# A12 B21 of a product of two weight matrices in seven inner products on top of A11 B11, and the products with B0 and G's in another order

## The chip, the cores and the metric

The kernel runs on one core of a Trainium2 chip (trn2). The metric is the device time in microseconds of one execution; a profiled execution gives in addition a trace, whose span runs from the first to the last instruction of the program. Engines are named as in the profile: PE is TensorE, PEld its weight loads, DVE is VectorE, ACT ScalarE, POOL GpSimd, SP the queue that issues most of the loads.

## The reference

`x` is 8 x 256 x 1024 in float32. Two layers follow each other, each adding a linear map and a low-rank one to its input:

```
x = x + x @ W0.T + 0.5 * (x @ A0[i0[b]]) @ B0.T
x = x + x @ W1.T + bias + 2.0 * (x @ A1[i1[b]]) @ B1[i1[b]]
```

W0 and W1 are 1024 x 1024. A0 is 5 x 1024 x 32, B0 1024 x 32, A1 32 x 1024 x 16, B1 32 x 16 x 1024; `i0` and `i1` hold an index for each batch.

## The kernel before

The kernel first builds M = (I + W0.T)(I + W1.T), a 1024 x 1024 product of the weights alone, and then multiplies each x by M. Everything is in float32. Both levels use a scheme with seven instead of eight block products (Strassen's, in Winograd's form). Outside, the weights are cut into blocks A11 to A22 and B11 to B22 of 512 x 512, and M comes out as m11, m12, m21, m22 (tiles of 128 x 4 x 512). The first two of the outer products are P1 = A11 B11 and P2 = A12 B21; m11 is their sum, and P1 is used for all the other blocks. `w_groups` holds one `Blocks` for each of the four row tiles of 128 rows; its methods `product6`, `product7`, `product5`, `product3` and `product4` make the other outer products of a row tile directly, four matmuls of 128 x 512 each. Row tiles 0 and 1 are done so, rows 2 and 3 by `Chain`, which makes its outer products in the inner form, seven products of 256 columns (`product`, `keep`, `form`, L515 to L594).

The inner form: `product` (L509 to L558 and around) takes four quarters of the left operand and sums of them (`z_sums`, four VectorE additions), and quarters of the right operand and sums of them (`Operand.sums`, four more). Each of its seven products is two matmuls of 128 x 256 into half a PSUM bank (`slot`); seven slots fill a set of four banks, `sets[0]` being banks 0 to 3 and `sets[1]` banks 4 to 7. Slots can be loaded beforehand and accumulated upon ("loaded"). `keep` copies a set out with four ACT copies, and `form` makes the four quarters of the result with five VectorE additions.

The work is put in order by hand (`manual_schedule`): each engine runs its instructions in the order of the program text, and waits for what each needs. At the start that order is:

- SP's queue: W1 comes as four blocks `wq[h, i]` of 512 x 512, each in four loads (the first in eight), W0 as eight row blocks in two halves of 512 columns (`load_w0(k, 0)`, then `load_w0(k, 1)`). The order is wq[0,0] with the first four W0 blocks between its halves, wq[0,1], the other four W0 blocks, wq[1,0], wq[1,1], `load_b0`, and the second halves of W0. "Third block" and "fourth block" below are wq[1,0] and wq[1,1].
- VectorE turns each block of W1 into `w1T` with stream transposes (`turn_w1`, L225) and adds the identity to the diagonals (L233; for h = 1 POOL does that).
- TensorE warms up with 15 matmuls (L918), makes P1 in two halves (`first`, L951) into banks 0 to 3, which ACT copies into m22 (`keep_p1`, L300), then P2 directly on top of the same banks (`product2`, 16 matmuls of 128 x 512, L286), which ACT copies into m11 (L310). Between these copies ACT issues the eight loads of A1's rows (`load_a1`, L198), three with each row tile.
- Then TensorE makes G = A1.T W0 in two halves (`prepare_down(h)`, L701), the product of B0 with W1 (`prepare_up`, L676, both halves, then `finish_up`, L690), the product of B0 and A1 (`prepare_cross`, L715), and goes on with `product6` of row tile 0. `finish_down` (L728 to L737) folds the cross product through bank 7, has ACT copy it out (L731), and transposes G in two fours of transposes, the second into bank 7.
- VectorE meanwhile makes the sums of the right operand, `sums_w1_first` (L359, L360), those of the left operand of row tile 0 (`w_groups[0].sums`, L272 to L279), and `sums_w1_last` (L365, L367). ACT then starts the inner sums of two right operands, `w_ops["t2"].sums_dma()` and `w_ops["t1"].sums_dma()`: three multiplications each (L431) into `units`, to which POOL's DMAs add.

Of the kernel before, what the change touches and what calls it, by code (L numbers as in the profile page):

```python
# [10 lines left out]
ALU = mybir.AluOpType  # L11
# [9 lines left out]
P = 128  # L21
NH = 512
# [5 lines left out]
NWARM = 15  # L28
NV7 = 7
# [3 lines left out]
NU = 2  # L33
NLOW = 4
NQ = NH // 2
NB = 4
NX = 2
# [5 lines left out]
def kernel(  # L43
# [179 lines left out]
    def turn_w1(wq, h: int, k: int, lo: int = 0, hi: int = NR):  # L223
        cols = slice(h * NH + lo * SQ, h * NH + hi * SQ)
        nc.vector.transpose(  # L225
            w1T[:, k, cols].rearrange("p (t q) -> p t q", q=SQ),
            wq[:, lo:hi].rearrange("p t (q m) -> p m t q", m=NB)[:, k % NB],
        )
# [18 lines left out]
    def new_bank():  # L247
        ring.append(ring.pop(0))
        return ring[-1]
# [225 lines left out]
    def quarters(x):  # L475
        return x[:, 0:2, 0:P], x[:, 2:4, 0:P], x[:, 0:2, P:T], x[:, 2:4, P:T]

    def z_sums(x, z):
        x11, x12, x21, x22 = x
        nc.vector.tensor_tensor(z[0], x21, x22, ALU.add)  # L480
        nc.vector.tensor_tensor(z[1], z[0], x11, ALU.subtract)
        nc.vector.tensor_tensor(z[2], x11, x21, ALU.subtract)
        nc.vector.tensor_tensor(z[3], x12, z[1], ALU.subtract)


    SLOT = {2: 0, 3: 1, 4: 2, 5: 3, 7: 4, 1: 5, 6: 6}
# [3 lines left out]
    def slot(ps, i: int):  # L490
        n, pos = BANK[i]
        return ps[n][:, pos * NQ : (pos + 1) * NQ]
# [78 lines left out]
    def form(v, ps=None, dst=None):  # L571
# [21 lines left out]
        nc.vector.tensor_tensor(mid, src_two(3, 0), two(1), ALU.add)  # L593
        nc.vector.tensor_tensor(d[:, 3 * NQ : 4 * NQ], src(5), at(6), ALU.add)  # L594

    m12 = {}

    def sums_m(m: int):
# [5 lines left out]
    class Chain:  # L604
# [33 lines left out]
            z_sums(self.q(name), self.z[name])  # L638

        def preload(self):  # L640

            p = m22[:, self.tiles, :].rearrange("p m (h n) -> p (m h) n", h=2)
            for i, part in ((2, 0), (4, 2), (5, 3)):
                nc.scalar.copy(slot(self.X, i), p[:, part])
            nc.vector.tensor_tensor(slot(self.X, 3), p[:, 1], p[:, 3], ALU.subtract)
            for i in (1, 7):
                nc.vector.memset(slot(self.X, i), 0.0)

        def product(self, ps, name, which, first, low=None):
            product(ps, self.q(name), self.z[name], w_ops[which], first, low=low)  # L650
# [14 lines left out]
            nc.vector.tensor_tensor(t[which], a, b, op)  # L665


    def prepare_up():
        tile = work[:, 4 * NH : 6 * NH]
        part = [tile[:, h * NH : (h + 1) * NH] for h in range(NO)]  # L670
        for h in range(NO):
            cols = slice(h * NH, (h + 1) * NH)
            pm = new_bank()
            for k in range(NK):
                g = k % 4
                nc.tensor.matmul(  # L676
                    pm[g * R0 : (g + 1) * R0, :],
                    b0[:, k, :],
                    w1T[:, k, cols],
                    start=(k < 4),  # L680
                    stop=(k >= NK - 4),
                )
            nc.scalar.copy(part[h], pm)
        return part

    def finish_up(part):
        for h in range(NO):
            cols = slice(h * NH, (h + 1) * NH)
            pm = new_bank()
            nc.tensor.matmul(  # L690
                pm, fold.rearrange("p u r -> p (u r)"), part[h], start=True, stop=True
            )
            for i in range(NU):
                nc.scalar.copy(ups[i][:, cols], pm)

    gT = [work[:, (6 + h) * NH : (7 + h) * NH] for h in range(NO)]

    def prepare_down(h: int):
        pm = new_bank()
        for k in range(NK):  # L700
            nc.tensor.matmul(  # L701
                pm,
                a1[:, k].rearrange("p b r -> p (b r)"),
                w0n[:, k, h * NH : (h + 1) * NH],
                start=(k == 0),
                stop=(k == NK - 1),
            )
        nc.scalar.copy(gT[h], pm)

    def prepare_cross():  # L710

        pe = banks[7][:, 0:P]
        for k in range(NK):
            g = k % 4
            nc.tensor.matmul(  # L715
                pe[g * R0 : (g + 1) * R0, :],
                b0[:, k, :],
                a1[:, k].rearrange("p b r -> p (b r)"),
                start=(k < 4),
                stop=(k >= NK - 4),  # L720
            )
        part = work[:, 4 * NH : 4 * NH + P]
        nc.scalar.copy(part, pe)
# [170 lines left out]
    with tc.manual_schedule(engines=ORDERED):  # L894
# [10 lines left out]
        load_w1(wq[0, 1], 0, 1)  # L905
        for k in range(NB, NK):
            load_w0(k, 0)
        for i in range(2):
            wq[1, i] = new_w1(1, i)
            load_w1(wq[1, i], 1, i)  # L910
        load_b0()
        for k in range(NK):
            load_w0(k, 1)
        nc.scalar.copy(s_all[:, 0:R0], ident[:, 0:R0])

        pw = banks[6][:, 0:P]
        for _ in range(NWARM):
            nc.tensor.matmul(pw, ident, ident, start=True, stop=True)  # L918
        raw0, raw1 = load_indices(idx0, 0), load_indices(idx1, 1)
        nc.gpsimd.memset(scale, L1_SCALING)  # L920
        for half in range(2):
# [27 lines left out]
        def first(g, k: int, n: int):  # L949
            cols = slice(n * NH // 2, (n + 1) * NH // 2)  # L950
            nc.tensor.matmul(  # L951
                g.p1[:, cols],
                g.a[0][:, k, :],
                w1T[:, k, cols],
                start=False,
                stop=(k == NB - 1),
                skip_group_check=True,
            )

        for k in range(NB):  # L960
            turn_w1(wq[0, 0], 0, k, 0, mid)
            diag_w0(k)
            for g in w_groups:
                first(g, k, 0)
        for k in range(NB):
            turn_w1(wq[0, 0], 0, k, mid, NR)
        for m, g in enumerate(w_groups):
            for k in range(NB):
                first(g, k, 1)
            g.keep_p1(m22[:, m, :])  # L970
        fixed0, fixed1 = fix_indices(raw0, N0, 0), fix_indices(raw1, N1, 1)
        for k in range(NB, NK):
            turn_w1(wq[0, 1], 0, k)
        for m, g in enumerate(w_groups):
            for b in range(3 * m, min(3 * m + 3, B)):
                load_a1(b)
            g.product2(m11[:, m, :])
        for k in range(NB):
            turn_w1(wq[1, 0], 1, k)
        for k in range(NB):  # L980
            turn_w1(wq[1, 1], 1, NB + k)
        for k in range(NB, NK):
            diag_w0(k)
        for k in range(NB):
            sums_w1_first(k)
        prepare_down(0)
        part = prepare_up()
        w_groups[0].sums()
        sums_w1_last()
        finish_up(part)  # L990
        prepare_down(1)
        prepare_cross()
        for which in ("t2", "t1"):
            w_ops[which].sums_dma()

# [285 lines left out]
```

## Time and profile before

| | us |
|---|---|
| median of 3 runs | 336.21 (335.87 to 336.40) |
| the profiled execution, its own time | 336.54 |
| its span | 334.8 |
| TensorE busy in the span | 329.6 (98%) |
| VectorE busy | 246.2 (74%) |
| ACT busy | 61.3 |
| POOL busy | 67.9 |

The granted TensorE clock was 0.999 of full speed. The stretch that the change touches lies between the start and 61 us. Busy times by engine there, from the view by windows: from 22.4 to 31.8 us TensorE was busy for 9.40, VectorE for 0.03; from 42.8 to 56.8, 14.00 and 13.79 us. A record of a float32 matmul in the trace is half of one matmul of the program, so 16 matmuls show as x32. "Busy" of TensorE includes the modelled end of a pipelined matmul; the time for one is best taken from a row of the chain, as its length over its count.

### The profile page before, as it was taken

To read this page: it belongs to the slowest core of one execution; us is meant where nothing else is said; L and a number is where in the kernel's file an instruction comes from. 1 tells how busy PE (TensorE), PEld (TensorE's weight loads), DVE (VectorE), ACT (ScalarE), POOL (GpSimd) and SP (SyncE) were. 2 spreads that over 40 slices of the span, in tenths; PEclk is the share of its full clock that TensorE was granted. 3 is DMA by queue.
4 is the path that set the end of the run, shared out by engine and by line. 5 is a ranking of instruction groups with operands and counts; after the bars stand their busy time and mean duration, and the time that the engine had idled before them with its cause. 6 is when DMAs were issued, how large, how long until landed. Compare 5 with 4: busy or idle time off the path is not lost.

```text
span 334.8 us, 4443 instructions
## 1 busy us (share of the span) xinstructions
PE 329.6 (98%) x1496; PEld 245.1 (73%) x1496; DVE 246.2 (74%) x466; ACT 61.3 (18%) x128; POOL 67.9 (20%) x125
## 2 busy tenths in 40 slices
PE   8999999999999999999999999999999999999996
PEld 8774434544488877888877887877888777788875
DVE  5752697159899999999997856985675986323964
ACT  1022043300034132440001330001331001322000
POOL 7001261540042232771023100012200010000000
PEclk9999999999999999999999999999999999999999
DMA  7949982990062980786277300275500121100113
GB/s 211 199 133 186 271 191 46 168 173 14 0 95 63 194 137 14 113 133 104 95 191 204 79 2 0 74 222 148 116 10 0 63 96 63 64 2 0 63 65 126
DMA packets 66399, 34.53 MB, mean 103 GB/s; under 512 B 47300, under 2 KB 61124, under 8 KB 66376
## 3 DMA queue, kind: packets, MB, share of 16 engines
q1 hardware_dynamic: 56520, 21.13, 27.9%
q0 software_dynamic: 7680, 12.59, 17.4%
q10 hardware_dynamic: 2176, 0.52, 1.0%
q8 instruction: 12, 0.20, 0.2%
q14 instruction: 11, 0.09, 0.1%
HBM read 19.55 MB, written 8.39 MB: 83 GB/s over the span
## 4 chain that ended last, share of the span: by engine, by line
PE 94%; DMA 2%; SPq 1%; DVE 1%; issue 0%; ACT 0%; DVEq 0%
PE bank L523 66%; PE bank L286 14%; PE bank L747 4%; PE bank L701 4%; DMA units<-in_L_cond_W_dram 2%; PE bank L951 2%; PE bank L676 1%; PE bank L765 1%; SPq L170 1%; DVE w1T L225 1%; PE bank L690 1%; SPq L178 1%; DVE w1T L233 0%; PE bank L736 0%; PE bank L715 0%
## 5 line engine op out<-in xcount | busy, mean ns | idle before, releaser
L509 DVE TENSOR_TENSOR work<-bank,work 128x512 f32<-128x512 f32 (+1 forms) x56 | 32.7, 620 | 19.0 <-PE bank L523 18.8
L505 ACT COPY work<-bank 128x512 f32<-128x512 f32 (+1 forms) x56 | 25.8, 548 | 43.0 <-PE bank L523 42.6
L225 DVE STREAM_TRANSPOSE w1T<-units 128x512 f32<-128x512 f32 (+1 forms) x20 | 17.3, 901 | 18.0 <-DMA units<-in_L_cond_W_dram 17.9
L888 POOL DMA_DIRECT2D out_dram<-work x12 | 9.0, 752 | 100.6 <-DVE work L594 100.6
L523 PE MATMUL bank<-w0n,w1T 128*128 128x256 f32 x104 | 24.6, 384 | 0.0
L755 ACT ACTIVATE a<-bank,shift,scale 128x256 f32<-128x256 f32 x8 | 4.5, 564 | 103.3 <-PE bank L747 103.3
L523 PEld LDWEIGHTS bank<-w0n,w1T 128*128 128x128 f32 x104 | 19.3, 190 | 4.1 <-issue 1.7
L523 PE MATMUL bank<-w0n,m 128*128 128x256 f32 x88 | 21.2, 384 | 0.0
L523 PE MATMUL bank<-w1T,s_all 128*128 128x256 f32 x80 | 20.2, 379 | 0.0
L238 DVE STREAM_TRANSPOSE units<-units 128x512 f32<-128x512 f32 x32 | 19.9, 676 | 0.2
L523 PEld LDWEIGHTS bank<-w0n,m 128*128 128x128 f32 x88 | 16.4, 190 | 3.4 <-issue 1.4
L523 PE MATMUL bank<-tw,m 128*128 128x256 f32 x68 | 17.5, 382 | 0.0
L523 PEld LDWEIGHTS bank<-w1T,s_all 128*128 128x128 f32 x80 | 15.2, 190 | 2.1
L523 PE MATMUL bank<-tw,s_all 128*128 128x256 f32 x64 | 16.1, 379 | 0.0
L747 PE MATMUL bank<-units,down 128*64 128x256 f32 x128 | 15.6, 385 | 0.0
L523 PE MATMUL bank<-m,units 128*128 128x256 f32 x64 | 15.1, 379 | 0.0
L951 PE MATMUL bank<-w1T,w0n 128*128 128x256 f32 x64 | 14.5, 383 | 0.5 <-DVE w1T L233 0.5
L523 PEld LDWEIGHTS bank<-tw,m 128*128 128x128 f32 x68 | 12.8, 190 | 2.4 <-issue 0.7
L523 PE MATMUL bank<-w0n,s_all 128*128 128x256 f32 x56 | 14.4, 379 | 0.0
L286 PE MATMUL bank<-tw,s_all 128*128 128x512 f32 x32 | 14.3, 595 | 0.0
L951 PEld LDWEIGHTS bank<-w1T,w0n 128*128 128x128 f32 x64 | 12.3, 196 | 2.4 <-DVE w1T L233 1.3
L701 PE MATMUL bank<-w0n,a 128*128 128x512 f32 x32 | 14.1, 592 | 0.0
(249 smaller groups left out, 646.8 us busy)
## 6 DMA issues: line engine op xcount, KB each, us to landing
units<-in_x_dram SPq DMA_DIRECT2D x128, 64.0 KB, 2.4
out_dram<-work POOLq DMA_DIRECT2D x12, 512.0 KB, 3.5
w0n<-in_L_cond_W_dram SPq DMA_DIRECT2D x16, 256.0 KB, 6.1
units<-in_L_cond_W_dram SPq DMA_DIRECT2D x12, 256.0 KB, 4.9
out_dram<-work SPq DMA_DIRECT2D x3, 512.0 KB, 3.2
units<-in_L_cond_W_dram SPq DMA_DIRECT2D x8, 128.0 KB, 4.6
down<-in_L_cond_lora_A_dram SPq DMA_DIRECT2D x32, 32.0 KB, 2.4
up<-in_L_cond_lora_Bs_dram SPq DMA_DIRECT2D x16, 64.0 KB, 2.7
```

The costliest lines, as they stand in the source:

```text
L170: nc.sync.dma_start(wq[g * SQ : (g + 1) * SQ, lo:hi, :], w1[rows, cols].rearrange("(t q) c -> q t c", q=SQ),)
L225: nc.vector.transpose(w1T[:, k, cols].rearrange("p (t q) -> p t q", q=SQ), wq[:, lo:hi].rearrange("p t (q m) -> p m t q", m=NB)[:, k % NB],)
L238: nc.vector.transpose(xT[:, NX * j : NX * (j + 1), :].rearrange("p c (t q) -> p c t q", q=SQ), xq[:, :, j, :].rearrange("p t (q c) -> p c ...
L286: nc.tensor.matmul(pm, a[:, k, :], b(k), start=first and k == 0, stop=(k == NB - 1), skip_group_check=not first,)
L505: nc.scalar.copy(at_home(v, n), whole(ps, n))
L509: nc.vector.tensor_tensor(at_home(v, n), whole(ps, n), at_home(v, n), ALU.add)
L523: nc.tensor.matmul(slot(ps, i) if dst is None else dst, lhs, rhs, start=BANK[i][0] not in started, stop=stop, skip_group_check=True,)
L701: nc.tensor.matmul(pm, a1[:, k].rearrange("p b r -> p (b r)"), w0n[:, k, h * NH : (h + 1) * NH], start=(k == 0), stop=(k == NK - 1),)
L747: nc.tensor.matmul(pl[half * MLOW : (half + 1) * MLOW, :], down[:, half * NB + k, :], x_b[half][:, k, :], start=(k == 0), stop=(k == NB - ...
L755: nc.scalar.activation(lows[:, b % NLOW], pl, mybir.ActivationFunctionType.Identity, bias=shift[:, 0:1], scale=scale[:, 0:1],)
L888: eng.dma_start(out[b, :, h * NH : (h + 1) * NH].rearrange("(j p) d -> p j d", p=P), ob[:, 0:D].rearrange("p (j d) -> p j d", d=NH),)
L951: nc.tensor.matmul(g.p1[:, cols], g.a[0][:, k, :], w1T[:, k, cols], start=False, stop=(k == NB - 1), skip_group_check=True,)
```

## The change

- P2 = A12 B21 is made in the inner form, for row tiles 0 and 1 together (`Second(0)`) and 2 and 3 together (`Second(1)`), in place of `product2`. P1 is copied into m22 as before and from there loaded into the slots: `load_inner` (three ACT copies), `load_inner_3` (one VectorE subtraction), `zero_inner` (two VectorE memsets). `Second(0)` uses banks 4 to 7, `Second(1)` banks 0 to 3. Products 1 and 2 of both come first, then the other five of each in the order 6, 5, 4, 7, 3. Each is kept in `units[0:2]` or `units[2:4]`, and `form` writes the result to m11.
- `z_sums` can do a part of its four sums.
- The two halves of `prepare_up` and `finish_up` are apart: `prepare_up(0)`, `prepare_down(0)`, `finish_up(0)`, `prepare_up(1)`, `prepare_down(1)`, `finish_up(1)`, `prepare_cross()`.
- On VectorE, `one.form()` stands between the turning of wq[1,0] and wq[1,1], `other.form()` behind `sums_w1_last()`. The fixing of the indices goes ahead of the second half of wq[0,0]'s turning.
- On ACT, two `a1` loads are issued behind row tile 1's `keep_p1`, six behind row tile 3's.
- On SP's queue, `load_b0` stands ahead of wq[1,0]; the second halves of W0 keep their place behind wq[1,1], and in the text stand behind `z_sums(other...)`.
- The 15 warming matmuls write banks 4 to 7 in place of one region of bank 6.

```diff
+    class Second:
+        op = Operand(
+            lambda j, n: w1T[:, NB + 2 * j : NB + 2 * j + 2, n * NQ : (n + 1) * NQ],
+            s_all[:, 0 : 4 * 2 * NQ].rearrange("p (i c n) -> p i c n", i=4, c=2),
+        )
+        def __init__(self, n: int):
+            self.tiles = slice(2 * n, 2 * n + 2)
+            self.ps = sets[1 - n]
+            a = w0n.rearrange("p k (j q c) -> p j k c q", j=NK // NX, c=NX)[:, n, NB:NK]
+            self.x = a[:, 0:2, 0], a[:, 2:4, 0], a[:, 0:2, 1], a[:, 2:4, 1]
+            z = s_all[:, (2 + n) * D : (3 + n) * D].rearrange("p (i c t) -> p i c t", i=4, c=2)
+            self.z = [z[:, i] for i in range(4)]
+            kept = units[:, 2 * n : 2 * n + 2].rearrange("p u n -> p (u n)")
+            self.kept = kept[:, 0 : NV7 * NQ]
+        def products(self, plan):
+            product(self.ps, self.x, self.z, self.op, "loaded", plan=plan)
+        def form(self):
+            form(self.kept, dst=m11[:, self.tiles, :].rearrange("p m n -> p (m n)"))
+
+    def load_inner(ps, tiles):
+        p = m22[:, tiles, :].rearrange("p m (h n) -> p (m h) n", h=2)
+        for i, part in ((2, 0), (4, 2), (5, 3)):
+            nc.scalar.copy(slot(ps, i), p[:, part])
+
+    def load_inner_3(ps, tiles):
+        p = m22[:, tiles, :].rearrange("p m (h n) -> p (m h) n", h=2)
+        nc.vector.tensor_tensor(slot(ps, 3), p[:, 1], p[:, 3], ALU.subtract)
+
+    def zero_inner(ps):
+        for i in (1, 7):
+            nc.vector.memset(slot(ps, i), 0.0)
...
         for k in range(NB, NK):
             load_w0(k, 0)
+        load_b0()
         for i in range(2):
             wq[1, i] = new_w1(1, i)
             load_w1(wq[1, i], 1, i)
-        load_b0()
-        for k in range(NK):
-            load_w0(k, 1)
...
+        fixed0, fixed1 = fix_indices(raw0, N0, 0), fix_indices(raw1, N1, 1)
         for k in range(NB):
             turn_w1(wq[0, 0], 0, k, mid, NR)
+        seconds = [Second(n) for n in range(2)]
+        one, other = seconds
+        zero_inner(one.ps)
         for m, g in enumerate(w_groups):
             for k in range(NB):
                 first(g, k, 1)
             g.keep_p1(m22[:, m, :])
-        fixed0, fixed1 = fix_indices(raw0, N0, 0), fix_indices(raw1, N1, 1)
+            if m % 2:
+                load_inner(seconds[m // 2].ps, seconds[m // 2].tiles)
+                for b in range(2) if m == 1 else range(2, B):
+                    load_a1(b)
         for k in range(NB, NK):
             turn_w1(wq[0, 1], 0, k)
-        for m, g in enumerate(w_groups):
-            for b in range(3 * m, min(3 * m + 3, B)):
-                load_a1(b)
-            g.product2(m11[:, m, :])
+        zero_inner(other.ps)
+        one.products([1, 2])
+        other.products([1, 2])
+        z_sums(one.x, one.z, 0, 2)
+        Second.op.sums()
+        z_sums(one.x, one.z, 2, 4)
+        load_inner_3(one.ps, one.tiles)
+        one.products([6, 5, 4, 7, 3])
+        keep(one.kept, one.ps)
+        load_inner_3(other.ps, other.tiles)
+        z_sums(other.x, other.z)
+        for k in range(NK):
+            load_w0(k, 1)
+        other.products([6, 5, 4, 7, 3])
+        keep(other.kept, other.ps)
+        prepare_up(0)
+        prepare_down(0)
         for k in range(NB):
             turn_w1(wq[1, 0], 1, k)
+        one.form()
         for k in range(NB):
             turn_w1(wq[1, 1], 1, NB + k)
         for k in range(NB, NK):
             diag_w0(k)
+        finish_up(0)
+        prepare_up(1)
+        prepare_down(1)
+        finish_up(1)
+        prepare_cross()
         for k in range(NB):
             sums_w1_first(k)
-        prepare_down(0)
-        part = prepare_up()
         w_groups[0].sums()
         sums_w1_last()
-        finish_up(part)
-        prepare_down(1)
-        prepare_cross()
+        other.form()
         for which in ("t2", "t1"):
             w_ops[which].sums_dma()
```

More of the change, by code (lines that the diff above doesn't have):

```diff
@@ L476, in quarters, with z_sums @@
         return x[:, 0:2, 0:P], x[:, 2:4, 0:P], x[:, 0:2, P:T], x[:, 2:4, P:T]
-    def z_sums(x, z):
+    def z_sums(x, z, first=0, last=4):
         x11, x12, x21, x22 = x
[L480 to L483, printed above, removed]
+        sums = (
+            (x21, x22, ALU.add),
+            (z[0], x11, ALU.subtract),
+            (x11, x21, ALU.subtract),
+            (x12, z[1], ALU.subtract),
+        )
+        for i in range(first, last):
+            nc.vector.tensor_tensor(z[i], *sums[i])
     SLOT = {2: 0, 3: 1, 4: 2, 5: 3, 7: 4, 1: 5, 6: 6}
@@ L594, in form @@
         nc.vector.tensor_tensor(d[:, 3 * NQ : 4 * NQ], src(5), at(6), ALU.add)
+    class Second:
+        op = Operand(
+            lambda j, n: w1T[:, NB + 2 * j : NB + 2 * j + 2, n * NQ : (n + 1) * NQ],
+            s_all[:, 0 : 4 * 2 * NQ].rearrange("p (i c n) -> p i c n", i=4, c=2),
+        )
+        def __init__(self, n: int):
[21 more added lines that the diff above has]
+            nc.vector.memset(slot(ps, i), 0.0)
     m12 = {}
@@ L640, in preload @@
         def preload(self):
[L642 to L647, printed above, removed]
+            load_inner(self.X, self.tiles)
+            load_inner_3(self.X, self.tiles)
+            zero_inner(self.X)
         def product(self, ps, name, which, first, low=None):
@@ L665, in sums_m, with prepare_up, finish_up @@
             nc.vector.tensor_tensor(t[which], a, b, op)
[L668 to L673, printed above, removed]
-            for k in range(NK):
[L675 to L689, printed above, removed]
-            nc.tensor.matmul(
-                pm, fold.rearrange("p u r -> p (u r)"), part[h], start=True, stop=True
-            )
-            for i in range(NU):
-                nc.scalar.copy(ups[i][:, cols], pm)
+    ups_parts = [work[:, (4 + h) * NH : (5 + h) * NH] for h in range(NO)]
+    def prepare_up(h: int):
+        pm = new_bank()
+        for k in range(NK):
+            g = k % 4
+            nc.tensor.matmul(
+                pm[g * R0 : (g + 1) * R0, :],
+                b0[:, k, :],
+                w1T[:, k, h * NH : (h + 1) * NH],
+                start=(k < 4),
+                stop=(k >= NK - 4),
+            )
+        nc.scalar.copy(ups_parts[h], pm)
+    def finish_up(h: int):
+        pm = new_bank()
+        nc.tensor.matmul(
+            pm, fold.rearrange("p u r -> p (u r)"), ups_parts[h], start=True, stop=True
+        )
+        for i in range(NU):
+            nc.scalar.copy(ups[i][:, h * NH : (h + 1) * NH], pm)
     gT = [work[:, (6 + h) * NH : (7 + h) * NH] for h in range(NO)]
@@ L910 @@
             load_w1(wq[1, i], 1, i)
-        load_b0()
-        for k in range(NK):
-            load_w0(k, 1)
         nc.scalar.copy(s_all[:, 0:R0], ident[:, 0:R0])
-        pw = banks[6][:, 0:P]
-        for _ in range(NWARM):
-            nc.tensor.matmul(pw, ident, ident, start=True, stop=True)
+        for n in range(NWARM):
+            bank, i = banks[4 + n // 4], n % 4
+            nc.tensor.matmul(
+                bank[:, i * P : (i + 1) * P],
+                ident,
+                ident,
+                start=(i == 0),
+                stop=True,
+                skip_group_check=True,
+            )
         raw0, raw1 = load_indices(idx0, 0), load_indices(idx1, 1)
@@ L970 @@
             g.keep_p1(m22[:, m, :])
-        fixed0, fixed1 = fix_indices(raw0, N0, 0), fix_indices(raw1, N1, 1)
+            if m % 2:
+                load_inner(seconds[m // 2].ps, seconds[m // 2].tiles)
+                for b in range(2) if m == 1 else range(2, B):
+                    load_a1(b)
         for k in range(NB, NK):
             turn_w1(wq[0, 1], 0, k)
-        for m, g in enumerate(w_groups):
-            for b in range(3 * m, min(3 * m + 3, B)):
-                load_a1(b)
-            g.product2(m11[:, m, :])
+        zero_inner(other.ps)
[9 more added lines that the diff above has]
+        z_sums(other.x, other.z)
+        for k in range(NK):
+            load_w0(k, 1)
[3 more added lines that the diff above has]
+        prepare_down(0)
         for k in range(NB):
             turn_w1(wq[1, 0], 1, k)
+        one.form()
         for k in range(NB):
```

## The prediction

> **What bounds the kernel now.** I read the page first. TensorE is busy for 329.6 of the 334.8 us of the profiled execution and holds 94% of the chain that ended last, so time that TensorE saves comes off the end, provided that nothing makes it wait. Next I read the chain of waits up to 110 us, where the change lies (columns: start, length, what):
>
> ```profile
> 16.43 5.89 PE bank L951 x26
> 22.32 13.73 PE bank L286 x32
> 36.05 6.87 PE bank L701 x16
> ...
> 55.85 3.63 PE bank L286 x8
> 59.48 0.23 PE bank L728 x2
> ...
> 59.74 0.25 ACT cross L731
> ...
> 60.00 0.27 ACT cross L731
> ...
> 60.31 0.74 PE bank L736 x4
> ```
>
> A12 B21 takes 13.73 us and ends at 36.05. Products with B0 and G's follow without a gap, then P6 of tile 0 (55.85). The only link off TensorE is at 59.74: two small ACT copies out of bank 7 (`finish_down`), on which the second four transposes, at 60.31, wait. Third, what stands before those copies in ACT's timeline, and how VectorE got there:
>
> ```profile
> 56.13 1.67 ACT L431 ACTIVATE units<-tw 128x512 f32<-128x512 f32 x3
> 57.70 1.65 ACT L431 ACTIVATE units<-w1T 128x512 f32<-128x512 f32 x3
> 59.74 0.52 ACT L731 COPY cross<-bank 32x128 f32<-32x128 f32 x2 [0.38 <-PE bank L728]
> ```
>
> ```profile
> 31.77 4.07 DVE L225 STREAM_TRANSPOSE w1T<-units 128x512 f32<-128x512 f32 x4 [9.41 <-DMA units<-in_L_cond_W_dram]
> 38.70 4.06 DVE L225 STREAM_TRANSPOSE w1T<-units 128x512 f32<-128x512 f32 x4 [2.85 <-DMA units<-in_L_cond_W_dram]
> ...
> 54.27 2.49 DVE L367 TENSOR_TENSOR tw<-w1T,tw 128x512 f32<-128x512 f32 x4
> ```
>
> ACT waits only 0.38 us for TensorE there. VectorE is idle for 9.41 us before the third block of W1, for 2.85 before the fourth, and from 38.70 it is busy without a gap to 56.76: that run starts when a load lands. Last, the queue that issues the loads, by its waits (total, times, longest):
>
> ```profile
> SPq L170 <- DMA work<-in_L_cond_lora_As_dram: 9.4, 2, 6.4
> ```
>
> SP's loads of W1 wait for ACT's loads of `a1` to land. In SP's timeline the first load of the third block is issued at 18.19, the second at 24.91, just after the first `a1` load (issued by ACT at 23.05, behind the four copies `keep_p1`) is in.
>
> **TensorE.** Removed: 32 records of 128x512 (16 matmuls, two records each), 13.73 us. Added: for each of two halves seven products of two 128x256 matmuls, 28 matmuls or 56 records. The L523 row of the chain (91.96, 18.13 us, x84) makes 0.216 us a record, so 12.1 us; the slower L951 row of the timeline (7.94 us, x36: 0.221) makes 12.4. I take 12.1, as L523 is the very code: **1.6 us less** (1.4 by the other). The 15 warming matmuls stay as many. The products with b0, a1 and fold are only reordered.
>
> Does it wait? Both halves' products 1 and 2 start at 22.32 and need only the turned B21 (VectorE 22.36) and the preloaded banks; 16 records end at 25.8. VectorE from 22.36: two memsets (0.27 each by L647), z0, z1 (0.45 and 0.34 apart in the run at 86.69), T3, T2 (0.72, 0.61 in the run at 95.13): T2 at 25.0, product 6 starts at 25.8. T1 and T4 at 26.3, z2 and z3 at 26.9, the preload of slot 3 at 27.3; product 4, which shares its bank, comes at 27.5. The other half's preload and four sums end at 29.2, TensorE is there at 30.1. So no stall, with 0.2 us to spare at the tightest place; if the preload is late, 0.4 us. The products end near 34.4 and TensorE reaches P6 at 54.2 instead of 55.85. `prepare_up(1)`, near 44, needs the fourth block turned with its diagonal by POOL (42.76 and 43.8 before): 0 to 0.3 us.
>
> **ACT.** `load_inner` adds 2 x 3 copies of 0.34 (L644), `keep` 2 x 4 (1.84 for four, L505), less four L310 copies of 0.58. The first two `a1` loads go ahead of the third `keep_p1`, at 0.9 us each on ACT (23.05, 24.02, 24.93): near 20.6 and 21.5 instead of 23.05. The last preload then ends near 24.1, when the other half's product 1 starts. All this lies under TensorE.
>
> **VectorE.** `zero_inner(one)` fits into the 0.89 us idle before 18.29, the index fixing (six small ones, 1.0 us, ending 17.4) into the 2.15 us idle before 12.50. Fourteen sums and preloads (6.3 us, 22.9 to 29.2) lie in the 9.41 us gap. `one.form()` (five instructions, 113.49 to 116.03: 2.54 us, the fourth done after 2.20) lies in the 2.85 us gap if the third block is turned by 35.84 as now. Without the cover it would cost its 2.5 us. `other.form()` has none: it comes after `sums_w1_last`, where VectorE has been busy since 38.70.
>
> **The wait that is added.** `other.kept` lies in `units[2:4]`, where the three ACT multiplications of `w_ops["t1"]` write. These must now wait for the fourth instruction of `other.form()`; behind them on ACT stand the cross copies, for which TensorE waits. With S the start of the fourth block's turning: `sums_w1_last` ends at S + 18.0 (56.7 - 38.7), form's fourth at + 2.2, three multiplications 1.67, two copies 0.53 and 0.07 of handing over: the second four transposes start at **S + 22.5**, but not before 60.31 - 1.6 = 58.7. The POOL transfers of t1 come no later than that with it; VectorE reads them at 78.64, 6 us after they land. VectorE's add of P6 slips to about 59.5; the bank that it frees is written next by P3, near 68. With S = 38.70 the transposes start at 61.2 instead of 60.31: **0.9 us slower**, the saved 1.6 us is spent as a wait.
>
> **S** is the open term. Down: ACT's first load is 2.4 us earlier, which would let SP go at 22.5 instead of 24.91. Then the third block lands 2.4 us earlier (29.2), turning (4.07) and form (2.54) end at 36.3: S = 36.3. Up: b0's 128 KB go first (about 0.3 us: it landed right behind the blocks); the other six `a1` loads are now issued in one run (24.4 to 29) instead of 26.3 to 30.8 between copies, and more of SP's loads wait for them; the last wait of that sort ended at 31.85. If the third block lands 1.4 us later by this, its form pushes S to 40.1 with no load late at all. I take S unchanged: the gain at the head is met by the burst behind it, and the form fills the gap (35.84 + 2.54 = 38.4, just under 38.70).
>
> On these loads the Trainium skill ("DMA: Bandwidth & Descriptors", Issuing engines are not separate DMA queues) states that starting DMAs from several engines saves no more than the sequencer's time to start them, as all run on the same 16 DMA engines. The row differs: 6.4 us of SP's queue hang on one ACT load while the DMA engines are nearly idle (0 GB/s from 22 to 24 us). By the rule the earlier ACT loads bring nothing and S is 38.7 or later; by the row up to 2.4 us. As to `one.form()` and POOL, "SBUF — State Buffer" (Who interferes with whom) has a VectorE instruction with two SBUF inputs and a GpSimd one that reads SBUF block one another fully. The trace shows VectorE at 0.9 to 1.0 us instead of 0.61 for five instructions from 43.37, beside POOL's diagonals; by the rule another 0.9 us would go (0.61 + 0.52 a pair, instead of 0.95) wherever more pairs met.
>
> **The sum.** Span 334.8: -1.6 us of matmuls, +2.5 us of waiting at the transposes = 335.7. The later stages are TensorE without a gap and VectorE fed by it, so I carry the difference to the end. The profiled execution's own time was 336.54, the median of the runs is 336.21; with the median: **337.1 us**.
>
> **The rivals.**
> *The loads come early (chance 0.33).* S is 36.3 to 38.1, and the result lies between -1.4 and +0.3 us. For: the 6.4 us wait. Against: the burst of six. It beats 0.2% where S falls below 37.2 (60.31 - 0.67 - 22.5 = 37.1): 334.8 to 335.5. About 0.25 for that.
> *TensorE starves or loads come late (0.2).* Order of landing is shared between SP and ACT; if the last W0 block of the first half (issued 16.68) falls behind the first `a1` load, it lands near 24.9, product 2 waits 1.3 us, the sums follow 1.8 us later; or the third block is late and S reaches 40: +1.5 to +2.7, 337.7 to 338.9. Against it: that load was out 6 us before.
> *The products save nothing (0.03).* Would need 0.245 us a record; no row of this width has it. 337.8 with S unchanged: the wait decides anyway.
> The forecast has the rest, 0.44, with +0.3 to +1.5 (336.5 to 337.7).
>
> **Range and chances.** A measurement of this kernel tells about 0.2% (0.67 us) from no change. Faster: 0.25, from the early loads. Within: 0.08 of these and 0.12 of the forecast, 0.20. Slower: the remaining 0.55. Range 334.9 to 338.9, from nearly the full saving to S near 40.3; less than 2 in 10 lie outside. The forecast's own is 336.5 to 337.7.
>
> **What would show it.** Right: ACT's L431 of w1T waits for VectorE's form, TensorE has a gap of 2 to 3 us before the second transposes; no gap in the products; their 56 records take 12.1 us; the fourth block's turning starts at 38 to 39. Wrong: no gap there and S below 37 (the rival of early loads), or a gap in the products near 23 us. I am wrong altogether if the form doesn't gate the multiplications.

## The result, and the profile after

The changed kernel takes 340.31 us in the median of four runs (339.75 to 340.83), beside 336.04 for the kernel before (335.87 to 336.40): a ratio of 1.0125, with an interval from 1.0106 to 1.0145. It is slower, as forecast, but by 4.3 us and not by 0.9; the time lies above the range. The profiled execution took 340.49 us, 3.95 more than the one before. First its page: the span, and the granted clock in 40 slices of 8.5 us.

```profile
span 338.7 us, 4535 instructions
...
PEclk9999999799999999999999999999999999999999
```

Before, every slice was 9. Now the eighth, from 59.3 to 67.7 us, has a 7. The chain of waits up to 110 us (start, length, what) passes through that slice:

```profile
25.58 4.72 DMA work<-in_L_cond_lora_As_dram
...
31.73 8.27 DMA units<-in_L_cond_W_dram
...
59.74 0.70 DVE m L597
60.47 1.67 ACT units L431 x3
62.13 0.14 ACT cross L765
62.29 0.27 ACT cross L765
62.60 1.02 PE bank L770 x4
63.62 32.30 PE bank L286 x72
95.92 14.24 PE bank L527 x66
```

Before, this chain lay on TensorE from 16 us on, but for two small copies. Now it comes from an `a1` load, over a W1 load that SP issued behind it and loads behind that, to VectorE's work up to the fourth instruction of `other.form()` (L597), and by ACT's three multiplications and the cross copies to the second four transposes (L770). (The loads in its middle are only one way back: in VectorE's timeline there is no idle time from 33.75 to 61.37 us, so what sets the end of that run is its beginning, the landing of the third block.) ACT's timeline shows the wait itself, behind the fourth instruction of the form:

```profile
60.47 1.67 ACT L431 ACTIVATE units<-w1T 128x512 f32<-128x512 f32 x3 [2.86 <-DVE m L597]
```

This wait, of ACT's multiplications for the form and so of TensorE for the cross copies behind them, is called the gate below. The differences to before follow from the starts and lengths. The transposes start at 62.60 instead of 60.31 (+2.29) and take 1.02 instead of 0.74 (+0.28); the 72 records of L286 take 32.30 instead of 30.90 (+1.40). That makes 3.97, and the next link starts 3.96 later (95.92 to 91.96). From there on the two traces run at a constant distance to the end.

TensorE's timeline (start, length, operation, count, in brackets the idle time before it and what ended it):

```profile
21.45 3.62 PE L527 MATMUL bank<-w1T,w0n 128*128 128x256 f32 x16
25.71 1.99 PE L527 MATMUL bank<-s_all 128*128 128x256 f32 x8 [0.64 <-DVE s_all L423]
28.02 1.14 PE L527 MATMUL bank<-s_all,w0n 128*128 128x256 f32 x4 [0.32 <-DVE bank L633]
...
35.13 1.92 PE L713 MATMUL bank<-w1T,b 128*32 128x512 f32 x16
...
59.02 0.64 PE L770 MATMUL bank<-ident,work 128*128 128x128 f32 x4
62.60 1.02 PE L770 MATMUL bank<-ident,work 128*128 128x128 f32 x4 [2.94 <-ACT cross L765]
63.41 5.04 PE L286 MATMUL bank<-tw,s_all 128*128 128x512 f32 x8
```

Before, the transposes were one piece, and the eight records behind them were shorter:

```profile
59.54 1.52 PE L736 MATMUL bank<-ident,work 128*128 128x128 f32 x8
60.89 3.60 PE L286 MATMUL bank<-tw,s_all 128*128 128x512 f32 x8
```

Three things are to be seen. The products of A12 B21 run from 21.45 to 35.13: 13.68 us, as long as the 13.73 of the old form, with two gaps in them. The wait at the transposes is 2.94 us. And the eight records behind it take 5.04 us where the same eight took 3.60 before.

VectorE's timeline shows where the first and the second come from:

```profile
22.64 0.27 DVE L637 MEMSET bank<- 128x256 f32 x1 [1.23 <-ACT bank L629]
23.25 0.27 DVE L637 MEMSET bank<- 128x256 f32 x1 [0.34 <-ACT bank L629]
...
33.75 4.25 DVE L225 STREAM_TRANSPOSE w1T<-units 128x512 f32<-128x512 f32 x4 [3.89 <-DMA units<-in_L_cond_W_dram]
...
40.35 4.06 DVE L225 STREAM_TRANSPOSE w1T<-units 128x512 f32<-128x512 f32 x4
```

The two memsets of the other half wait for ACT's preload (L629), 1.57 us together. The third block of W1 is turned from 33.75 instead of 31.77, and S, the start of the fourth block's turning, is 40.35 instead of 38.70. No load ended the time before S: VectorE came straight from `one.form()`.

### The profile page after: what moved, and what is told of

The parts are those of the page before. It is cut to its first block, busy times and chain, and to the rows that moved or that the text cites. A ratio compares the mean times of both kernels' runs of the same rounds, so it can differ in the third digit from the quotient of the medians.

```text
span 338.7 us, 4535 instructions
## 1 busy us (share of the span) xinstructions
PE 329.7 (97%) x1520; PEld 249.5 (74%) x1520; DVE 258.1 (76%) x494; ACT 64.4 (19%) x138; POOL 68.7 (20%) x125
## 4 chain that ended last, share of the span: by engine, by line
PE 85%; DMA 6%; DVE 3%; POOL 1%; SPq 1%; ACT 1%; issue 1%; ACTq 1%; POOLq 0%
PE bank L527 65%; PE bank L286 10%; PE bank L781 4%; PE bank L991 4%; DMA units<-in_L_cond_W_dram 2%; DMA w0n<-in_L_cond_W_dram 2%; DMA work<-in_L_cond_lora_As_dram 1%; PE bank L799 1%; SPq L155 1%; DVE tw L367 1%; DVE w1T L365 1%; DMA units<-in_x_dram 1%; ACT units L431 0%; SPq L170 0%; POOL idx L128 0%
## 5 line engine op out<-in xcount | busy, mean ns | idle before, releaser
L527 PE MATMUL bank<-w1T,s_all 128*128 128x256 f32 x88 | 22.3, 379 | 0.0
L527 PEld LDWEIGHTS bank<-w1T,s_all 128*128 128x128 f32 x88 | 16.7, 190 | 2.3
L286 PE MATMUL bank<-tw,s_all 128*128 128x512 f32 x32 | 15.8, 645 | 0.0
```

The lines of the kernel that those rows point to most:

```text
L286: nc.tensor.matmul(pm, a[:, k, :], b(k), start=first and k == 0, stop=(k == NB - 1), skip_group_check=not first,)
L527: nc.tensor.matmul(slot(ps, i) if dst is None else dst, lhs, rhs, start=BANK[i][0] not in started, stop=stop, skip_group_check=True,)
```

## The experiments

In each, only what the diff shows differs from the changed kernel (e11: from the kernel before). Ratios are to the kernel before, run beside it. S is as in the prediction; "products" is the time from the first product of A12 B21 to the first record behind them.

| | S, us | products, us | wait at the second transposes, us | median, us | ratio and its interval |
|---|---|---|---|---|---|
| before | 38.70 | 13.73 | none | 336.04 | |
| after | 40.35 | 13.68 | 2.94 | 340.31 | 1.0125 (1.0106 to 1.0145) |
| e1 t1 behind the cross copies | 41.73 | 13.65 | none | 336.36 | 1.0008 (0.9994 to 1.0022) |
| e3 matmuls in the wait | 40.46 | 13.65 | filled | 339.63 | 1.0104 (1.0082 to 1.0126) |
| e5 a1 by SP | 35.96 | 13.65 | none | 336.13 | 1.0000 (0.9985 to 1.0014) |
| e6 both e1 and e5 | 36.40 | 13.65 | none | 336.03 | 1.0009 (0.9995 to 1.0023) |
| e7 e1, all of a1 last | 42.67 | 13.84 | none | 337.55 | 1.0043 (1.0028 to 1.0057) |
| e8 old order of B0 and G | 40.39 | 13.65 | 2.44 | 340.75 | 1.0142 (1.0128 to 1.0155) |
| e9 e6, sums first | 35.20 | 12.18 | none | 334.62 | 0.9961 (0.9948 to 0.9975) |
| e10 sums first alone | 37.71 | 12.18 | 1.35 | 336.61 | 1.0030 (1.0010 to 1.0049) |
| e11 before, a1 by SP | 34.34 | 13.73 | none | 335.73 | 0.9995 (0.9987 to 1.0004) |
| e12 e9, old order of B0 and G | 35.11 | 12.09 | none | 334.11 | 0.9952 (0.9938 to 0.9966) |

**e1: take away what the transposes wait for.** The multiplications of `w_ops["t1"]` are put behind the cross copies, so that `other.form()` gates nothing on TensorE's path.

```diff
-        for which in ("t2", "t1"):
-            w_ops[which].sums_dma()
+        w_ops["t2"].sums_dma()
...
         finish_down()
+        w_ops["t1"].sums_dma()
```

> The changed kernel with one move: the inner sums of t1 (three ACT multiplications and their DMAs) are started behind finish_down instead of ahead of it. Nothing is left out. Theory A (the loss is the wait of ACT's multiplications for other.form, behind which the cross copies stand): the second four transposes no longer wait 2.9 us, start near 59.7 instead of 62.6, TensorE's next products run at full pace, and the time falls by some 4.5 us against the changed kernel, to 335.3 to 336.2, ratio to before 0.997 to 1.000, although the fourth block is still turned only at 40.35. Theory B (the late third block itself costs the time, by whatever comes next): 339 to 340.5, and another wait takes the place.

Measured: 336.36 us, 0.2 above the range expected by theory A. In TensorE's timeline the eight transposes are one piece again, and the records behind them have their old length:

```profile
45.30 2.58 PE L713 MATMUL bank<-w1T,b 128*32 128x512 f32 x16
...
60.06 1.52 PE L770 MATMUL bank<-ident,work 128*128 128x128 f32 x8
61.41 3.60 PE L286 MATMUL bank<-tw,s_all 128*128 128x512 f32 x8
```

All of the loss is gone with the wait, though S is even later here (41.73). What the later block costs without the gate is seen in the first line: `prepare_up(1)` needs it and takes 2.58 us instead of 1.92. The gain that the new form was to bring is not there either: its products still take 13.65.

**e3: keep the wait, keep TensorE busy in it.** Thirteen matmuls of the identity with itself are issued between the two fours of transposes. They write bank 5, so what later products accumulate there is changed.

```diff
             pt = (banks[7] if h else low_bank()).rearrange(...)
+            for n in range(13 * h):
+                nc.tensor.matmul(
+                    banks[5][:, 0:P], ident, ident, start=True, stop=True
+                )
```

> The changed kernel with 13 matmuls of ident by ident into the free bank 5 between the two fours of transposes, in the 2.9 us in which TensorE waits. Nothing is left out, but work without use is added. Theory A (TensorE's granted clock falls after the wait: the two products behind it take 5.04 us instead of 3.60): the wait is the same, the transposes start at 62.6, the product behind them takes 3.6, and the time falls by 1.4 us to 338.6 to 339.3. Theory B (the slow product has another cause than the idle time): no change or slower, 340 to 341.

Measured: 339.63 us. The transposes start as late as before, but what follows is faster:

```profile
59.59 3.07 PE L769 MATMUL bank<-ident 128*128 128x128 f32 x26
62.75 0.74 PE L774 MATMUL bank<-ident,work 128*128 128x128 f32 x4
63.33 3.60 PE L286 MATMUL bank<-tw,s_all 128*128 128x512 f32 x8
```

0.74 and 3.60 us are the lengths of the kernel before. So the 1.02 and 5.04 of the changed kernel are the idle time's second price. The granted clock says the same. From the view by windows of the changed kernel (window, its length, busy time and count for each engine; then the granted clock, the DMA share and GB/s):

```profile
59.00:62.60 3.60, 0.66 (x6) 0.47 (x4) 2.32 (x4) 2.10 (x6) 1.56 (x3) 1.00 1.09 154
62.60:65.00 2.40, 2.40 (x6) 1.49 (x7) 0.00 (x0) 1.43 (x3) 2.17 (x2) 0.56 0.96 183
65.00:68.00 3.00, 3.00 (x7) 1.39 (x6) 0.00 (x0) 0.00 (x0) 0.00 (x0) 0.78 1.19 191
```

The clock is 0.56 and 0.78 of full speed in the two windows behind the idle time: 2.40 x 0.44 + 3.00 x 0.22 = 1.7 us of work lost, the 0.28 + 1.40 of the chain. In e3 both windows have 1.00. At 162 us e3 is 1.5 us ahead of the changed kernel; at 164 us 0.65 of that is lost, where its TensorE waits for a sum of VectorE's (L437) and the changed kernel's, coming later, does not. This fits the 0.7 us in the median, half of what was expected. One of the changed kernel's own four runs had a mean clock of 1.000 instead of 0.995, and it is the fastest, 339.75.

**e2 and e4: the `a1` loads through POOL's queue**, to part them from SP's and ACT's; e4 has e1's edit as well.

```diff
-        j = index(fixed1, b, N1, mybir.EngineType.Activation)
-        nc.scalar.dma_start(
+        j = index(fixed1, b, N1, mybir.EngineType.Pool)
+        nc.gpsimd.dma_start(
...
-        fixed0, fixed1 = fix_indices(raw0, N0, 0), fix_indices(raw1, N1, 1)
         for k in range(NB):
             turn_w1(wq[0, 0], 0, k, mid, NR)
...
         zero_inner(one.ps)
+        fixed0, fixed1 = fix_indices(raw0, N0, 0), fix_indices(raw1, N1, 1)
```

> The changed kernel with a1's rows loaded by POOL's queue instead of ACT's; the index fixing back behind the second half of the first block's turning, so that these loads are not ahead of W1's second block. Nothing is left out. Theory A (SP's loads hang on the landing of ACT's a1 loads, which makes the third block late; form then pushes the fourth): SP issues the third and fourth blocks from 18 us without the 6.4 us wait, they land near 27 and 34, the fourth is turned from about 35.5 (S), the transposes could start at S + 22.5 = 58.0 and TensorE doesn't wait there; the products lose their gaps; time 333.8 to 334.8, ratio 0.993 to 0.996. Theory B (the DMA engines' throughput sets the landing; b0 ahead and the shared DMA engines are what is late): the blocks land at 32 and 39 as now, 338.5 to 340.5.

> e1 and e2 together. Theory A: as e2 if no wait is left there, 333.8 to 334.8 (0.993 to 0.996), since with the early fourth block the order of t1 and the cross copies no longer matters. If the blocks are still late: as e1, 335.3 to 336.2.

Measured: 360.84 us (1.0737, 1.0716 to 1.0758) and 361.13 us (1.0745, 1.0721 to 1.0770). The times do not answer the question, since I had overlooked that POOL also copies each loaded row block (L202), and stands in its queue until the load is in. (The traces answer half of it: SP has no wait for an `a1` load, the third block is turned from 29.66 in e2 and 30.21 in e4 without idle time before it, and S is 36.12 and 36.70.) The eight loads went one after another; POOL's timeline in e2:

```profile
26.48 0.51 POOL L202 COPY a<-work 128x128 f32<-128x128 f32 x1 [7.08 <-DMA work<-in_L_cond_lora_As_dram]
34.25 0.32 POOL L202 COPY a<-work 128x128 f32<-128x128 f32 x1 [6.08 <-DMA work<-in_L_cond_lora_As_dram]
...
57.46 0.29 POOL L202 COPY a<-work 128x128 f32<-128x128 f32 x1 [1.49 <-DMA work<-in_L_cond_lora_As_dram]
```

G's first product had to wait for the last of them, and the clock shows again what idle time does, in e2 and then in e4:

```profile
57.80 8.64 PE L735 MATMUL bank<-w0n,a 128*128 128x512 f32 x16 [20.77 <-POOL a L202]
```

```profile
59.14 9.57 PE L735 MATMUL bank<-w0n,a 128*128 128x512 f32 x16 [21.55 <-POOL a L202]
```

These 16 records take 7.13 us in the changed kernel: 1.5 us for the clock in e2 and 2.4 us in e4, behind idle times of 20.8 and 21.6 us, beside 1.7 behind one of 2.9.

**e5 and e6: the `a1` loads on SP's own queue**, between the third and the fourth block; e6 has e1's edit as well.

```diff
-        j = index(fixed1, b, N1, mybir.EngineType.Activation)
-        nc.scalar.dma_start(
+        j = index(fixed1, b, N1)
+        nc.sync.dma_start(
...
-        for i in range(2):
-            wq[1, i] = new_w1(1, i)
-            load_w1(wq[1, i], 1, i)
+        wq[1, 0] = new_w1(1, 0)
+        load_w1(wq[1, 0], 1, 0)
...
         fixed0, fixed1 = fix_indices(raw0, N0, 0), fix_indices(raw1, N1, 1)
+        for b in range(B):
+            load_a1(b)
+        wq[1, 1] = new_w1(1, 1)
+        load_w1(wq[1, 1], 1, 1)
...
-                for b in range(2) if m == 1 else range(2, B):
-                    load_a1(b)
```

> The changed kernel with a1's eight loads on SP's own queue, between the third and the fourth block of W1, and none on ACT; everything else as in the changed kernel, nothing left out. Theory A (SP's loads hang on ACT's a1 loads, and the fourth block's turning at S + 22.5 sets the second transposes): no 6.4 us wait on SP, the third block lands near 27, the fourth near 35, S about 36.3 (third turned from 29.9, then form), so the transposes could start at 58.8, hardly later than TensorE comes; ACT's preloads are no longer behind loads and the products lose the 0.6 us gap. Wait at the transposes 0 to 0.5 us, time 333.3 to 334.8, ratio 0.992 to 0.997. Theory B (DMA throughput makes the blocks late whatever the queue): third block 32 to 34, S 39 to 40, 338 to 340.

> a1's loads on SP's queue as in the run before this, and t1's inner sums behind finish_down as in the first run. Theory A: as the run before or up to 0.5 us faster, 333.0 to 334.5. If the blocks are still late: as the first run, 336.0 to 336.8.

Measured: 336.13 and 336.03 us. VectorE's timeline in e5:

```profile
29.53 4.08 DVE L225 STREAM_TRANSPOSE w1T<-units 128x512 f32<-128x512 f32 x4
...
35.96 4.10 DVE L225 STREAM_TRANSPOSE w1T<-units 128x512 f32<-128x512 f32 x4
```

With the `a1` loads out of ACT's queue the third block is there before VectorE is free, S is 4.4 us earlier and the wait is gone although the multiplications stand where they stood. So the lateness of the third block comes with the `a1` loads on ACT, and the changed kernel's row of SP's waits names it (total, times, longest):

```profile
SPq L170 <- DMA work<-in_L_cond_lora_As_dram: 10.4, 3, 6.4
```

Before, it was 9.4 us in two waits. But both runs miss their expected time, by 1.3 us and more: the gaps within the products are still there (0.61 and 0.32 us), and with them the 1.5 us that I had counted on.

**e7: are the gaps ACT's `a1` loads?** e1's edit, and all eight loads behind the second preload, so that no load stands between ACT's copies.

```diff
-                for b in range(2) if m == 1 else range(2, B):
+                for b in range(B) if m == 3 else ():
                     load_a1(b)
```

> The first run's kernel (t1 behind finish_down), and all eight a1 loads on ACT behind the preload of the second half, instead of two of them ahead of row tile 2's copy. Theory A (the 0.6 us gap at product 6 comes from these two loads, which delay ACT's copies, the memsets and T2): the memsets run right behind the turning, T2 is ready 1 us earlier, the gaps of 0.6 and 0.3 us in the products are gone; SP's first wait ends near 24 to 25 as before. Time 335.3 to 336.0 (0.998 to 1.000) if the third block isn't later than in the first run. Theory B (the gaps come from VectorE's sums themselves): the gaps stay, 336.0 to 336.8.

Measured: 337.55 us, above the ranges of both theories, and gaps of 0.61 and 0.51 us. They are not the loads' doing; as in e5, the memsets wait for ACT's preload (0.61 and 0.34 us). The third block is turned only at 36.10: SP's load of `b0`, which stands ahead of the block's, waits 8.6 us for an `a1` load.

**e9: VectorE's work in another order.** e6, and the memsets of the other half go ahead of ACT's preload of the same banks, and the preload of slot 3 goes right behind T2.

```diff
-            if m % 2:
-                load_inner(seconds[m // 2].ps, seconds[m // 2].tiles)
+            if m == 1:
+                load_inner(one.ps, one.tiles)
...
         zero_inner(other.ps)
+        load_inner(other.ps, other.tiles)
...
         z_sums(one.x, one.z, 0, 2)
-        Second.op.sums()
-        z_sums(one.x, one.z, 2, 4)
+        Second.op.sums(0, 2)
         load_inner_3(one.ps, one.tiles)
+        Second.op.sums(2, 4)
+        z_sums(one.x, one.z, 2, 4)
```

> The kernel with a1 on SP's queue and t1 behind finish_down, and in addition the order at the start of the products changed: the memsets of the second half's slots come ahead of ACT's preload of the same banks instead of behind it, and the preload of slot 3 of the first half comes right behind T2. Nothing is left out. Theory A (the saving of the seven products, 1.6 us, is lost in two gaps in the products, because VectorE's memsets wait for ACT's preload of the same banks, so that T2 and slot 3 come late): VectorE starts its sums 1 us earlier, both gaps go, the products take 12.1 to 12.4 us instead of 13.65, and the time falls by 1.2 to 1.5 us against that kernel, to 334.4 to 335.0, ratio 0.9955 to 0.9975. Theory B (256-column products cost more than their rows say): the products take over 13 us without gaps, ratio 0.999 to 1.002.

Measured: 334.62 us. TensorE's timeline:

```profile
21.56 3.62 PE L531 MATMUL bank<-w1T,w0n 128*128 128x256 f32 x16
25.02 1.89 PE L531 MATMUL bank<-s_all 128*128 128x256 f32 x8
26.74 1.03 PE L531 MATMUL bank<-s_all,w0n 128*128 128x256 f32 x4
...
33.74 1.92 PE L717 MATMUL bank<-w1T,b 128*32 128x512 f32 x16
```

No gap is left, and the products take 33.74 - 21.56 = 12.18 us: the 12.1 of the prediction. The memsets start at 21.58 without a wait. (`sums` of the operand is only given bounds, so that it can be made in two parts.) e9 is faster than the kernel before by 0.4%.

**e10: the order of e9 alone**, on the changed kernel, with `a1` on ACT (two loads behind the first preload, six behind the second) and the gate in its place.

> The changed kernel with this order at the start of the products alone: a1 stays on ACT, t1 ahead of finish_down. Theory A (the second transposes wait for ACT, ACT for other.form, and that stands S + 22.5 after the start of the fourth block's turning): TensorE comes 1.2 to 1.5 us earlier to the transposes and waits that much longer; the time stays within 0.5 us of the changed kernel, 339.8 to 341.0. Theory B (TensorE's work sets the time there): 338.7 to 339.2.

Measured: 336.61 us, 3 us less than expected. I had held S fixed, and it moved. VectorE's and TensorE's timelines:

```profile
31.09 4.19 DVE L225 STREAM_TRANSPOSE w1T<-units 128x512 f32<-128x512 f32 x4 [2.14 <-DMA units<-in_L_cond_W_dram]
...
37.71 4.07 DVE L225 STREAM_TRANSPOSE w1T<-units 128x512 f32<-128x512 f32 x4
```

```profile
60.00 0.75 PE L774 MATMUL bank<-ident,work 128*128 128x128 f32 x4 [1.35 <-ACT cross L769]
60.58 3.60 PE L286 MATMUL bank<-tw,s_all 128*128 128x512 f32 x8
```

The third block landed 2.7 us earlier: SP's first load of it goes out at 21.95 us instead of 24.59, and its waits for `a1` loads are four instead of three, the longest 5.2 us instead of 6.4, though both kernels issue the same loads in the same order on each queue, and ACT at much the same times (its two groups of them begin at 20.00 and 23.26 instead of 19.51 and 22.77). Why the waits fell otherwise stays open. Some of the difference is there before the first `a1` load: SP issues `b0` at 16.39 instead of 17.79. The gate held: S + 22.5 = 60.2, measured 60.00. A wait of 1.35 us left the clock at full speed (3.60 us for the eight records). Of its twelve runs, two have a mean clock of 0.995, at 337.84 and 339.14 us, against 335.71 for the fastest; that S varies from run to run would explain it, but only one of the twelve, at 336.22 us and full clock, has a trace.

**e8, e12: the order of the products with B0 and G**, put back as before, in the changed kernel (e8) and in e9 (e12).

```diff
-        prepare_up(0)
         prepare_down(0)
...
-        finish_up(0)
-        prepare_up(1)
-        prepare_down(1)
-        finish_up(1)
+        prepare_up(0)
+        prepare_up(1)
+        finish_up(0)
+        finish_up(1)
+        prepare_down(1)
         prepare_cross()
```

> The changed kernel with the products of B0 and G's in the order of before (first part of G's, both parts of B0's, the rest). Nothing is left out. Theory A (the transposes wait for ACT, and that for VectorE's S + 22.5): TensorE waits 1 to 2 us for the fourth block in B0's product, comes later to the transposes and waits there correspondingly less; they start at 62.6 as now and the time is the same within 0.4 us, or up to 1 us shorter where the shorter wait leaves the clock up: 339.2 to 340.6. Theory B (the order of the products matters by itself): the wait for the fourth block is added, 341 to 342.5.

> As the first kernel of this group, but the products of B0 and G's in the order of before. Theory A (with the early fourth block nothing in B0's product waits, so that the order is free): within 0.3 us of that kernel, 334.3 to 335.2. Theory B (the new order of the products is needed, or costs, by itself): off by more than 0.5 us.

Measured: 340.75 us, between the ranges of the two theories, and 334.11 us, just under the range of theory A. e8 meets the same gate: S is 40.39, the transposes start at 62.77, and 4.89 us for the eight records behind the wait show the clock again. The order of the products is not what made the kernel slower, and it is not free either: from the first record behind the products to P6 of tile 0 it is 53.45 - 33.57 = 19.88 us in e12 and 53.87 - 33.74 = 20.13 in e9, where B0's product is in two parts. e12, the new form of A12 B21 without the gate, the late loads, the gaps and the new order, is the fastest of all: 0.5% less than the kernel before.

**e11: the control.** The kernel before with `a1` on SP's queue, as in e5.

> The kernel before with a1's loads on SP's queue between the third and the fourth block, as a control: nothing else is changed. Theory A (earlier blocks are of use only where the form must fit in behind the third one; before the change TensorE waits for no block): third block near 27, fourth near 35, time as before, 335.7 to 336.3. Theory B (earlier blocks help by themselves): 0.5 us or more faster.

Measured: 335.73 us, not told apart from no change, with S at 34.34. Before the change an earlier block brings nothing. A later one has its price through the gate, and a small one in `prepare_up(1)` (0.66 us in e1).

## Why the prediction was right or wrong

**The gate was right, in place and in size.** The prediction had the second transposes at S + 22.5 wherever `other.form()` decides. Put in 40.35, it makes 62.85; measured 62.60. In e3 and e8 it makes 62.96 and 62.89 (62.75 and 62.77 measured), in e10 60.2 (60.00). Its parts hold too: `sums_w1_last` ends at S + 18.0 (55.82 + 2.49 - 40.35), the fourth instruction of the form 2.1 us later, the multiplications take 1.67. e1 shows that this wait is what made the kernel slower.

**"S unchanged" failed; it was the first of two terms that made the loss larger than forecast.** I set the gain of ACT's earlier first loads against the burst behind them and took nothing. In fact the third block landed 2.0 us later, VectorE went from its turning through `one.form()` into the fourth block without a pause, and S was 1.65 us late. The working had this case: a third block 1.4 us late would push S to 40.1 "with no load late at all". (By its own terms, 35.84 + 1.4 + 2.54, it is 39.8; with the 2.0 us measured it is 40.4, as seen. The S of the early loads, given as 36.3, is likewise 36.0: 31.77 - 2.4 + 4.07 + 2.54.) I priced it inside the rival of late loads with a chance of 0.2, and the place and the delay at the transposes (+2.29, within that rival's +1.5 to +2.7) came out as there. That the block is late with `a1` on ACT and not with `a1` on SP's queue is shown by e5.

How the 2.0 us came about is seen in SP's timeline, of which these are the block's four loads before:

```profile
18.19 0.33 SPq L170 DMA_DIRECT2D units<-in_L_cond_W_dram  x1
24.91 1.39 SPq L170 DMA_DIRECT2D units<-in_L_cond_W_dram  x3
```

and after, with `b0` ahead of them:

```profile
17.79 0.39 SPq L188 DMA_DIRECT2D b<-in_L_cond_lora_B_w_dram  x1
24.59 0.86 SPq L170 DMA_DIRECT2D units<-in_L_cond_W_dram  x2
28.81 0.84 SPq L170 DMA_DIRECT2D units<-in_L_cond_W_dram  x2
```

Before, one load was out ahead of the wait and the other three followed at 24.91. Now `b0` is what goes out ahead of it. The gain at the head did not come: SP's wait ends at 24.59, when ACT's third load is in (POOL copies it at 24.63), although the first two were in by 23.07. And the burst was not free: the block's last two loads wait until 28.81, when another load of the burst is in (copied at 28.84). How much of the 2.0 us is `b0`'s place and how much the burst's was not tried, and stays open. The two together need not make the block late: e10 has both, its four loads go out at 21.95, 24.24, 24.61 and 26.27, and the block is turned from 31.09, earlier than before the change (31.77).

**The clock was not in the prediction at all; it was the second term.** I priced the wait as its length. It cost 1.7 us more at the place, by the clock, and the sum of all terms at 95.9 us is +0.89 for the gate with the old S, +1.65 for S, -0.25 for the gate's own error and +1.68 for the clock: 3.97. Not all of the clock's part need reach the end: in e3 0.65 of the 1.5 us was lost again on the way.

The Trainium skill ("TensorE: Matmul & The Clock Gate", What's actually happening) states that TensorE runs at half its clock after at least one idle window of some 3.4 us, and at full clock again after a window of work. I had weighed no such rule against my own wait. The recovery agrees in part: half speed for 3.4 us would cost an estimated 1.7 us, as measured here, with 1.5 in e2 but 2.4 in e4. The idle time does not: here 2.94 us by the profile, and 2.44 in e8, sufficed; 1.35 us in e10 did not lower it.

**"So no stall" failed, at no cost here.** The records' price was right (12.18 us in e9 and 12.1 predicted), but 1.5 us of the saving went into gaps. What failed is "VectorE from 22.36: two memsets (0.27 each)". I had ACT's preload ending near 24.1 and noted it only as a matter for the other half's product 1. The memsets write the other halves of the banks that ACT is loading, and stand behind that preload in the program. So they and all sums behind them came about 1.6 us later, T2 is ready 4.2 us after the first product instead of 2.7, and product 6 waits for it; slot 3's preload, behind eight sums, does the rest. The Trainium skill ("PSUM — Partial Sum Buffer", PSUM bank collisions raise a hardware error) states that two engines must not be in one bank, on the same partitions, at the same time, on whatever columns; by it such a wait can be turned round, as in e9, but not dropped. The rows agree: the memsets wait 1.23 and 0.34 us for copies into the other half. The tightest place was given 0.2 us to spare, in a sum that left out such a wait. In the changed kernel the gate hid this loss, since a saving ahead of a gate only makes the wait longer; it is why e1 and e5 end level with the kernel before, and e9's order is what turns e6's 336.03 into 334.62.

**Reordering costed at nothing** was off by 0.25 us (e9 and e12, one trace each). That VectorE and ACT had room otherwise held. That the later stages carry a difference to the end held between the two kernels, but not for all of e3's gain.

## What to carry to other kernels

When a new instruction is put ahead of a long run on an engine, find the start of that run and what sets it before anything else; here S decided how long TensorE waited, and it was taken as unchanged. When a wait like these, of 2.4 us or more on TensorE, is foreseen, price the clock behind it too, or keep TensorE at work. And when VectorE and ACT fill one PSUM bank, each in its half, the order of the two in the program is a wait of its own: put the short one first.

## What was not expected of the hardware

- The clock falls behind a short idle time: 0.56 of full speed in the 2.4 us behind an idle time of 2.94 us, 0.78 in the next 3.0, then 1.00: some 1.7 us of work lost. Behind idle times seven times as long it was of the same order, 1.5 us (e2, 20.8 us idle) and 2.4 (e4, 21.6).
- The landing of one block varies widely with the loads on other queues: the third block of W1 was turned at 25.78, 29.53, 31.09, 33.75 and 36.10 us in e11, e5, e10, the changed kernel and e7, which issue the same loads. It is not their order alone: in e10, the changed kernel and e1 (35.15) that is the same on each queue.
- Loads through POOL's queue go one by one where POOL itself waits for each: the last of eight was copied at 57.5 us in e2, and at 30.9 us in the changed kernel.
